# Rotary attention: a tile's three projections one behind the other, and the steps' instructions bound to the order in the source

## The chip, the cores and the metric

The kernel runs on one core of a Trainium2 chip. The metric is device time in microseconds (us), the median of several runs. The core has five engines that work side by side, each with its own queue of instructions in a fixed order: TensorE (PE in the profile, its weight loads PEld), VectorE (DVE), ScalarE (ACT), GpSimd (POOL) and SyncE (SP), which here issues transfers. A dependency between engines is a semaphore: an instruction whose input is late holds back everything behind it in its engine's queue. Results of TensorE go to PSUM, a small memory that is handed out in buffers. TensorE's clock is granted by a throttle; the profile shows it as a share of full speed (PEclk).

## What is computed

A residual stream x of 32 sequences, each 64 x 256, goes through eight blocks, alternately a form of attention or mixing and a form of feed-forward network; each adds its gated result to x. The seventh, called block 6 here since counting starts at 0, is an attention with rotary positions over 64 channels (8 heads of 8) and 256 positions, with keys and values from a second input c:

```python
def _L3_xattn_ref(x, c, Wq, bq, Wk, bk, Wv, bv, Wo, bo):
    ...
    q = split_heads(_proj(x, Wq, bq))
    k = split_heads(_proj(c, Wk, bk))
    v = split_heads(_proj(c, Wv, bv))
    q = _apply_rotary(q_emb, q)
    k = _apply_rotary(k_emb, k)
    scores = jnp.einsum('bhtc,bhsc->bhts', q, k) / math.sqrt(K_CH)
    p_attn = jax.nn.softmax(scores, axis=-1)
    out = jnp.einsum('bhts,bhsc->bhtc', p_attn, v)
    ...
    return _proj(out, Wo, bo)
...
x = x + jnp.tanh(g_xattn[3]) * _L3_xattn_ref(_layernorm(x, axis=-1), ctx_2048, ...)
x = x + jnp.tanh(g_ffn[3]) * _L3_ffn_ref(_layernorm(x, axis=-1), L3_ffn_W1, L3_ffn_W2, L3_ffn_W3)
```

The last line is block 7, a feed-forward network whose hidden values pass a Walsh-Hadamard transform; the kernel applies the transform to the weights W2 in place of the hidden values.

## The kernel before

x stays on the chip as 16 tiles of 128 rows, two sequences each. `block6` (L1102) is a generator: each `yield` ends a step, and there are 4 x 32 + 12 = 140 steps, numbered g = 0 to 139. A sequence takes four steps of scores, so a tile takes eight, and the steps are a software pipeline over several sequences:

- `start(i)` (L1150) prepares tile i: the layer norm xn (DVE), the key projection pk (8 matmuls of L1161 on ctx, into a PSUM pair), two multiplies by cosine and sine (t, L1164, DVE), their sum k and two masked copies kb (L1170, L1173, POOL); then the query projection pq from xn (also L1161) with its two multiplies and the sum q (L1177, POOL); then the value projection pv, into a small PSUM buffer of the pool `aux`, and copies into va (ACT). It yields after each of the three, and the loop at the end of `block6` takes these parts at steps with g % 8 = 1, 5 and 7, for the tile that comes next.
- `scores(w, p, g)` (L1200) does two score groups in one step. For the sequence that starts now, pp (L1219, 4 matmuls) holds scores with queries on the partitions, and DVE takes their negated maxima (mx, L1227). For the sequence six steps older, pw (L1211, 8 matmuls) holds the scores with keys on the partitions and the maximum already inside, and ACT takes the exponential e (L1223).
- `shift` (L1193) turns the four steps' maxima (pt) and adds them to the query (qs, DVE); `mix` (L1229) multiplies e with the values (po) and is called twice a sequence; `normalise` (L1239) transposes (pn), takes the reciprocal and the product o (DVE); `turn` (pot, L1251) and `finish` (py, L1258) make the output projection, and POOL adds it to x (L1263). A sequence reaches them 4, 8, 10, 11, 13 and 15 steps after its start.

PSUM limits how far steps overlap. pw, pp and the key and query projections all take a `pair` (L1127), a buffer of two banks. There are two such buffers, and a third from step 7 on; they are taken in turn, so a new pair waits until the third last one has been read.

The layer norm's mean and variance (`_stats`, L112; one `bn_stats` of L98 and one aggregate of L101 a tile, and an inverse root by 11 small operations for four tiles together) are asked for four tiles at a time: at the beginning for tiles 0 to 3, and then, in the source, one tile a step over four steps and the inverse root whole in the fifth, 14 steps ahead of each further group of four.

Steps 0 to 6 are laid between the last pieces of block 5, two steps to three pieces. The remaining ones run in the loop of `program` at L1505. That loop also takes pieces of `weights7` (L1309) at every fourth step from g = 60 on: four Hadamard products of weights (ph, PE and ACT), then butterflies of additions and subtractions on POOL between ha and hb (L1326, L1327). At g = 130 it calls `next(seventh)`, which runs `features(0)` of block 7 (L1341): statistics of tiles 0 to 3, four normalised tiles xn, eight transposes (L153) and two copies xf, with which block 7's first matmuls begin.

The order of the source is not the order of the queues. The language's scheduler takes the program's instructions and places each on its engine's queue by its own estimate of readiness; what a later block's source asks for can come to lie between the instructions of an earlier one, as long as the dependencies hold. Tiles are handed out from their pools accordingly.

Of the kernel before, what the change touches and what calls it, by code (L numbers as in the profile page):

```python
# [17 lines left out]
F32 = mybir.dt.float32  # L18
# [8 lines left out]
P = 128  # L27
B, S, D = 32, 64, 256
# [52 lines left out]
def _rsqrt(c, pool, nv, tag, bufs=1):  # L81


    nc = c.nc
    n = nv.shape[1]
    r, t = (pool.tile([P, max(n, 4)], F32, tag=f"{tag}_{m}", name=f"{tag}_{m}", bufs=bufs)[:, :n] for m in "rt")
    nc.vector.tensor_scalar(r.bitcast(I32), nv.bitcast(I32), -0.5, GUESS, ALU.mult, ALU.add)
    for _ in range(3):
        nc.vector.tensor_tensor(t, r, r, ALU.mult)
        nc.vector.tensor_tensor(t, t, nv, ALU.mult)  # L90
        nc.vector.scalar_tensor_tensor(r, t, 1.5, r, ALU.add, ALU.mult)
    return r

# [10 lines left out]
def _inverse(c, pool, mv, tag, bufs=1):  # L104

    n = mv.shape[1]
    nv = pool.tile([P, max(n, 4)], F32, tag=f"{tag}_nv", name=f"{tag}_nv", bufs=bufs)[:, :n]
    c.nc.vector.tensor_scalar(nv, mv[:, :, 1], 1e-5, -0.5, ALU.add, ALU.mult)
    return _rsqrt(c, pool, nv, tag, bufs)

# [991 lines left out]
def block6(c):  # L1102
# [7 lines left out]
    nc = c.nc  # L1110
    HN, HC = 8, 8
# [8 lines left out]
    with ExitStack() as es:  # L1120
# [29 lines left out]
        def start(i):  # L1150

            xn = _norm(c, tp, lns[i // 4], i, bufs=2)
            ctx = c.ctx.rearrange("p k t -> p (k t)")[:, i * D : (i + 1) * D]

            def project(w, src, n):

                pp = pair("pp")
                for r in range(2):
                    for m in range(2):
                        rows = slice(m * S, (m + 1) * S)  # L1160
                        nc.tensor.matmul(pp[:, m, r, :], w[rows, r, :], src[rows, :], start=True, stop=True)  # L1161
                t = [tp.tile([P, 2, D], F32, tag=f"t{r}", name=f"t{r}") for r in range(2)]
                for r, f in enumerate((cos, sin)):
                    nc.vector.scalar_tensor_tensor(t[r], pp[:, :, r, :], bias[:, n, r : r + 1], f, ALU.add, ALU.mult)  # L1164
                return t

            a = [SimpleNamespace(i=i, n=n, e={}, mx=mxs[n]) for n in range(2)]
            t = project(wk, ctx, 1)
            k = tp.tile([P, 2, D], F32, tag="k", name="k", bufs=1)
            nc.gpsimd.tensor_tensor(k, t[0], t[1], ALU.add)  # L1170
            kb = tp.tile([P, 2, 2, D], F32, tag="kb", name="kb", bufs=3)
            for h in range(2):
                nc.gpsimd.tensor_scalar(kb[:, :, h, :], k, odd[:, h : h + 1], None, ALU.mult)  # L1173
            yield a
            t = project(wq, xn, 0)
            q = tp.tile([P, 2, D], F32, tag="q", name="q", bufs=3)
            nc.gpsimd.tensor_tensor(q, t[0], t[1], ALU.add)  # L1177
            yield a
            pv = ps1.tile([P, 2, P], F32, tag="a", name="pv")
            for j in range(2):  # L1180
                nc.tensor.matmul(pv[:, j, :], ctx[:, j * P : (j + 1) * P], wv, start=True, stop=True)
            va = vas[i % 3]
            o = tp.tile([P, 2, 2, S], F32, tag="o", name="o")
            for n in range(2):
                src = pv[:, :, n * S : (n + 1) * S].rearrange("p k (h d) -> p k h d", d=HC)
                nc.scalar.copy(va[:, n, :, :, :HC], src)
                a[n].q, a[n].k, a[n].v, a[n].o = q[:, n], kb[:, n], va[:, n], o
            yield a
# [77 lines left out]


        lns = [_stats(c, sm, 0, 4, bufs=2)]
        seqs = []
        for g in range(4 * B + 12):  # L1270
            at = lambda back: seqs[(g - back) // 4] if g >= back and (g - back) // 4 < B else None
            first = lambda back: at(back) if (g - back) % 4 == 0 else None
            if g == 0:
                seqs += list(start(0))[-1]
            scores(at(6), at(0), g)
            if a := first(8):
                mix(a, 0)
# [8 lines left out]
            if (a := first(15)) and a.n:  # L1286
                finish(a)
            if g // 8 + 1 < B // 2 and g % 8 in (1, 5, 7):
                if g % 8 == 1:
                    parts = start(g // 8 + 1)  # L1290
                fresh = next(parts)
                if g % 8 == 7:
                    seqs += fresh

            ahead = g - 32 * len(lns) + 14
            if len(lns) < 4 and ahead >= 0:
                if ahead == 0:
                    mv = sm.tile([P, 4, 2], F32, tag="ln_mv", name="ln_mv", bufs=2)
                if ahead < 4:
                    _mean(c, sm, mv[:, ahead, :], 4 * len(lns) + ahead)  # L1300
                else:
                    lns.append((mv, _inverse(c, sm, mv, "ln", 2), 4 * len(lns)))
            yield
# [72 lines left out]
def program(tc, a, out):  # L1376
    nc = tc.nc
    with ExitStack() as es:
# [122 lines left out]
        with ExitStack() as es6:  # L1501
            c.third = es6.enter_context(tc.tile_pool(name="ps6b", bufs=1, space=PSUM))
            ha = es6.enter_context(tc.tile_pool(name="ha7", bufs=1)).tile([P, NH, D], F32, tag="ha", name="ha")
            w2s = weights7(c, ha, hb)
            for _ in sixth:  # L1505
                if g >= 60 and g % 4 == 0:
                    next(w2s, None)
                if g == 4 * B + 2:
                    next(seventh)
                g += 1  # L1510
        next(seventh, None)
# [119 lines left out]
```

## Time and profile before

| quantity | value |
|---|---|
| median of 3 runs | 1457.77 us (1457.44 to 1458.16) |
| profiled execution | 1453.52 us |
| its span | 1451.7 us |
| mean granted TensorE clock | 0.934 |
| block 6's exps (L1223) | 128 of 1.024 us each |
| block 6's maxima (L1227) | 128 of 1.219 us each |
| eight matmuls of one projection (L1161) | 1.06 us from the first one's start to the next group's |
| first matmul of block 7 (L1361) | at 1279.45 us |

The span goes from the first to the last instruction of the profiled execution; its own time, 1453.52 us, has 1.8 us around that. In the profile's rows the arrow `pw<-qs,kb` says that an instruction writes pw from qs and kb; x with a number is how many instructions are put together; brackets give the idle time of the engine just before, and what ended it. The timeline's columns are start, length, engine, line, operation, names and shapes. The windows give, for a stretch of time, the busy time of each engine with its number of instructions, the granted clock, the share of the transfer engines and what they moved.

### The profile page before, as it was taken

The page shows a single profiled execution, that of the slowest core. Times are in us where ns is not written, and L with a number is a line of the kernel's source. Part 1 is how long each engine was busy: PE and PEld are TensorE (multiplying, and loading weights), DVE is VectorE, ACT ScalarE, POOL GpSimd, SP SyncE. Part 2 cuts the span into 40 slices and gives each one's busy share as a digit, 9 for nine tenths or more (in the row PEclk, how much of TensorE's full clock was granted, in tenths as well). Part 3 has the DMA queues.
Part 4 walks back from the last instruction along what each step waited for, and adds up shares of the span by engine and source line. Part 5 has one row for each costly group of instructions (what it writes and reads, how often), then busy time and mean ns, then how long its engine had stood idle before and what let it go on. Part 6 is the DMA issues. An engine that isn't in the chain of part 4 may idle for free.

```text
span 1451.7 us, 21390 instructions
## 1 busy us (share of the span) xinstructions
PE 1265.6 (87%) x8342; PEld 745.8 (51%) x8342; DVE 930.1 (64%) x2189; ACT 619.1 (43%) x1044; POOL 448.9 (31%) x466
## 2 busy tenths in 40 slices
PE   1889989999879999778888874899899899999999
PEld 1666445455223677555555552455455455546665
DVE  5679685643378877686888778677776677532111
ACT  2554451312311455566777762255455354531110
POOL 3352442301131323344555455233135332100000
PEclk9999999999999999887998887699899899999999
DMA  5000000100530200000000010200000000000000
GB/s 202 15 7 9 1 1 11 48 0 8 196 116 1 95 1 1 1 1 1 2 1 1 1 60 0 87 2 1 1 2 1 1 1 2 1 0 15 15 15 14
DMA packets 10293, 34.12 MB, mean 24 GB/s; under 512 B 1360, under 2 KB 5968, under 8 KB 8528
## 3 DMA queue, kind: packets, MB, share of 16 engines
q1 hardware_dynamic: 10192, 32.76, 6.3%
q8 instruction: 65, 1.06, 0.3%
q14 instruction: 36, 0.29, 0.1%
HBM read 30.66 MB, written 2.10 MB: 23 GB/s over the span
## 4 chain that ended last, share of the span: by engine, by line
PE 55%; DVE 25%; POOL 9%; issue 4%; ACT 4%; DMA 2%; SPq 0%; POOLq 0%; DVEq 0%; ACTq 0%
PE pw L1211 5%; PE po L1371 4%; PE pg L1361 4%; PE pu L1361 4%; PE pp L1219 4%; PE pc L581 4%; PE po L1234 3%; POOL kb L1173 2%; DVE mx L1227 2%; PE pq L806 2%; PE pu L434 2%; PE pg L434 2%; PE pm L1061 2%; PE pu L437 2%; DMA w<-in_l2f 2%
## 5 line engine op out<-in xcount | busy, mean ns | idle before, releaser
L1223 ACT ACTIVATE e<-pw 128x1024 f32<-128x1024 f32 x128 | 131.0, 1024 | 175.5 <-PE pp L1219 171.5
L1227 DVE TENSOR_REDUCE mx<-pp 128x4 f32<-128x1024 f32 x128 | 156.0, 1219 | 77.4 <-PE pp L1219 77.4
L1211 PE MATMUL pw<-qs,kb 32*128 32x256 f32 x1024 | 159.0, 415 | 7.0 <-DVE mx L1227 7.0
L1219 PE MATMUL pp<-kb,q 32*128 32x512 f32 x512 | 153.7, 676 | 7.5 <-DVE mx L1227 5.0
L1211 PEld LDWEIGHTS pw<-qs,kb 32*128 32x128 f32 x1024 | 88.3, 188 | 49.5 <-issue 26.6
L581 PE MATMUL pc<-xw,wb 64*64 64x512 f32 x768 | 93.3, 619 | 0.2 <-DVE x L514 0.2
L440 ACT ACTIVATE sg<-pg 128x512 f32<-128x512 f32 (+1 forms) x75 | 37.8, 511 | 115.9 <-PE pg L434 50.5
L98 DVE BATCH_NORM_STATS2 ln_st<-x 128x6 f32<-128x256 f32 x128 | 51.0, 411 | 38.2 <-POOL x L1263 27.6
L1364 DVE TENSOR_TENSOR h<-pu,sg 128x512 f32<-128x512 f32 x32 | 22.1, 691 | 80.8 <-PE pu L1361 80.8
L441 DVE TENSOR_TENSOR h<-pu,sg 128x512 f32<-128x512 f32 (+1 forms) x75 | 42.5, 573 | 48.3 <-PE pu L434 30.0
L1234 PE MATMUL po<-e,va 128*32 128x256 f32 x1024 | 70.6, 395 | 1.2 <-ACT e L1223 1.2
L1363 ACT ACTIVATE sg<-pg 128x512 f32<-128x512 f32 x32 | 19.1, 597 | 122.8 <-PE pg L1361 122.7
L732 POOL TENSOR_TENSOR acc<-acc,sq 128x512 f32<-128x512 f32 x28 | 39.4, 1408 | 69.8 <-ACT sq L731 68.4
L581 PEld LDWEIGHTS pc<-xw,wb 64*64 64x64 f32 x768 | 29.8, 138 | 59.6 <-issue 58.8
L1361 PE MATMUL pg<-xf,wa 128*128 128x512 f32 x128 | 60.3, 592 | 0.0
L1361 PE MATMUL pu<-xf,wa 128*128 128x512 f32 x128 | 60.3, 592 | 0.0
L1170 POOL TENSOR_TENSOR k<-t,t 128x512 f32<-128x512 f32 x16 | 20.3, 1266 | 123.4 <-DVE t L1164 123.4
L1371 PE MATMUL po<-hb,h 128*128 128x256 f32 x256 | 55.9, 379 | 0.0
L1066 POOL TENSOR_TENSOR v<-v,wb 128x512 f32<-128x512 f32 x32 | 40.6, 1274 | 42.7 <-ACT v L1065 42.5
L1371 PEld LDWEIGHTS po<-hb,h 128*128 128x128 f32 x256 | 48.6, 190 | 8.3 <-issue 1.9
L139 DVE TENSOR_SCALAR xn<-x,ln_mv,ln_r 128x256 f32<-128x256 f32 x112 | 49.5, 474 | 4.9 <-PE pt L153 4.1
L1219 PEld LDWEIGHTS pp<-kb,q 32*128 32x128 f32 x512 | 41.0, 192 | 22.4 <-DVE mx L1227 16.5
(337 smaller groups left out, 3012.8 us busy)
## 6 DMA issues: line engine op xcount, KB each, us to landing
w<-in_l2f SPq DMA_DIRECT2D x12, 512.0 KB, 4.4
wa<-in_l0f SPq DMA_DIRECT2D x2, 1828.0 KB, 12.2
wa<-in_l1f SPq DMA_DIRECT2D x2, 1536.0 KB, 9.2
wa<-in_l3f SPq DMA_DIRECT2D x2, 1536.0 KB, 8.1
wb<-in_conv SPq DMA_DIRECT2D x1, 2048.0 KB, 7.6
ctx<-in_ctxT SPq DMA_DIRECT2D x2, 1024.0 KB, 6.2
ctx<-in_ctxN SPq DMA_DIRECT2D x2, 1024.0 KB, 6.0
out<-x SPq DMA_DIRECT2D x16, 128.0 KB, 1.7
```

The costliest lines, as they stand in the source:

```text
L98: ins = c.nc.vector.bn_stats(st, c.x[:, i, :])
L139: c.nc.vector.tensor_scalar(xn, c.x[:, i, :], mv[:, j, 0:1], rs[:, j : j + 1], ALU.subtract, ALU.mult)
L434: nc.tensor.matmul(p, wt[:, k, fc], xf[:, k, :N], start=k == 0, stop=False, skip_group_check=True)
L441: nc.vector.tensor_tensor(h[s][:, f, :], pu, sg, ALU.mult)
L581: nc.tensor.matmul(pcs[h][to], w[rows, k, m, h, :], xw[rows, k, h, :, Z - m : Z - m + 32], start=m == 0, stop=m == Z)
L1211: nc.tensor.matmul(pw[:, jj, k, :], w.k[rows, h, k * P : (k + 1) * P], w.qs[rows, :], start=True, stop=True)
L1219: nc.tensor.matmul(pp[:, jj], p.q[rows, t * P : (t + 1) * P], p.k[rows], start=True, stop=True)
L1223: nc.scalar.activation(e, pw, AF.Exp, scale=scale)
L1227: nc.vector.tensor_reduce(p.mx[:, t, i0 : i0 + 2, 16:18], pp, AX.X, ALU.max, negate=True)
L1234: nc.tensor.matmul(po[strip(j), :], a.v[:, k, 2 * j + h, :], a.e[h, j][:, k, :], start=k == 0, stop=k == 1)
L1361: nc.tensor.matmul(p, wt[:, k, fc], xf[:, k, :], start=k == 0, stop=k == 1)
L1371: nc.tensor.matmul(po, h[:, f, q * P : (q + 1) * P], c.w2h[:, f, :], start=f == 0, stop=f == NH - 1)
```

## The change

The projections of a tile are issued together. `start(i)` yields once after its layer norm, taken at g % 8 = 1, and then does pk, pv and pq directly one behind the other at g % 8 = 3, right after that step's scores and ahead of its `mix`, `shift`, `normalise`, `turn` and `finish`. The value projection takes a `pair` in place of the small buffer. The multiplies, sums and copies follow the three.

The statistics come in single pieces: `stats6` does one tile, or one round of the inverse root, a step; it begins 18 steps ahead of its group's first step in place of 14.

The loop over the rest of block 6, with the pieces of `weights7` and the call of `next(seventh)`, stands in `tc.manual_schedule` for PE, DVE, ACT and POOL: these engines' instructions from there keep the order of the source. SP is not in the list. No operation is added or left out.

```diff
@@ -81,15 +81,21 @@
 def _rsqrt(c, pool, nv, tag, bufs=1):
+    return [r for r in _rsqrt_slowly(c, pool, nv, tag, bufs)][-1]
+
+
+def _rsqrt_slowly(c, pool, nv, tag, bufs=1):
+
     nc = c.nc
     n = nv.shape[1]
     r, t = (pool.tile([P, max(n, 4)], F32, tag=f"{tag}_{m}", name=f"{tag}_{m}", bufs=bufs)[:, :n] for m in "rt")
     nc.vector.tensor_scalar(r.bitcast(I32), nv.bitcast(I32), -0.5, GUESS, ALU.mult, ALU.add)
     for _ in range(3):
+        yield None
         nc.vector.tensor_tensor(t, r, r, ALU.mult)
         nc.vector.tensor_tensor(t, t, nv, ALU.mult)
         nc.vector.scalar_tensor_tensor(r, t, 1.5, r, ALU.add, ALU.mult)
-    return r
+    yield r
 def _mean(c, pool, mv, i, here=False):
@@ -103,10 +109,14 @@
 def _inverse(c, pool, mv, tag, bufs=1):
+    return [r for r in _inverse_slowly(c, pool, mv, tag, bufs)][-1]
+
+
+def _inverse_slowly(c, pool, mv, tag, bufs=1):
     n = mv.shape[1]
     nv = pool.tile([P, max(n, 4)], F32, tag=f"{tag}_nv", name=f"{tag}_nv", bufs=bufs)[:, :n]
     c.nc.vector.tensor_scalar(nv, mv[:, :, 1], 1e-5, -0.5, ALU.add, ALU.mult)
-    return _rsqrt(c, pool, nv, tag, bufs)
+    yield from _rsqrt_slowly(c, pool, nv, tag, bufs)
 def _stats(c, pool, i0=0, n=NT, bufs=1, here=False):
@@ -1149,41 +1159,48 @@
         def start(i):
+
             xn = _norm(c, tp, lns[i // 4], i, bufs=2)
             ctx = c.ctx.rearrange("p k t -> p (k t)")[:, i * D : (i + 1) * D]
-
-            def project(w, src, n):
+            yield
+
+            def project(w, src):
                 pp = pair("pp")
                 for r in range(2):
                     for m in range(2):
                         rows = slice(m * S, (m + 1) * S)
                         nc.tensor.matmul(pp[:, m, r, :], w[rows, r, :], src[rows, :], start=True, stop=True)
+                return pp
+
+            def rotate(pp, n):
+
                 t = [tp.tile([P, 2, D], F32, tag=f"t{r}", name=f"t{r}") for r in range(2)]
                 for r, f in enumerate((cos, sin)):
                     nc.vector.scalar_tensor_tensor(t[r], pp[:, :, r, :], bias[:, n, r : r + 1], f, ALU.add, ALU.mult)
                 return t
             a = [SimpleNamespace(i=i, n=n, e={}, mx=mxs[n]) for n in range(2)]
-            t = project(wk, ctx, 1)
+            pk = project(wk, ctx)
+            pv = pair("pv").rearrange("p a b d -> p (a b d)")[:, : 2 * P].rearrange("p (j o) -> p j o", j=2)
+            for j in range(2):
+                nc.tensor.matmul(pv[:, j, :], ctx[:, j * P : (j + 1) * P], wv, start=True, stop=True)
+            pq = project(wq, xn)
+            va = vas[i % 3]
+            for n in range(2):
+                src = pv[:, :, n * S : (n + 1) * S].rearrange("p k (h d) -> p k h d", d=HC)
+                nc.scalar.copy(va[:, n, :, :, :HC], src)
+            t = rotate(pk, 1)
             k = tp.tile([P, 2, D], F32, tag="k", name="k", bufs=1)
             nc.gpsimd.tensor_tensor(k, t[0], t[1], ALU.add)
             kb = tp.tile([P, 2, 2, D], F32, tag="kb", name="kb", bufs=3)
             for h in range(2):
                 nc.gpsimd.tensor_scalar(kb[:, :, h, :], k, odd[:, h : h + 1], None, ALU.mult)
-            yield a
-            t = project(wq, xn, 0)
+            t = rotate(pq, 0)
             q = tp.tile([P, 2, D], F32, tag="q", name="q", bufs=3)
             nc.gpsimd.tensor_tensor(q, t[0], t[1], ALU.add)
-            yield a
-            pv = ps1.tile([P, 2, P], F32, tag="a", name="pv")
-            for j in range(2):
-                nc.tensor.matmul(pv[:, j, :], ctx[:, j * P : (j + 1) * P], wv, start=True, stop=True)
-            va = vas[i % 3]
             o = tp.tile([P, 2, 2, S], F32, tag="o", name="o")
             for n in range(2):
-                src = pv[:, :, n * S : (n + 1) * S].rearrange("p k (h d) -> p k h d", d=HC)
-                nc.scalar.copy(va[:, n, :, :, :HC], src)
                 a[n].q, a[n].k, a[n].v, a[n].o = q[:, n], kb[:, n], va[:, n], o
             yield a
@@ -1265,14 +1282,27 @@
+        def stats6(i0):
+            mv = sm.tile([P, 4, 2], F32, tag="ln_mv", name="ln_mv", bufs=2)
+            for j in range(4):
+                _mean(c, sm, mv[:, j, :], i0 + j)
+                yield
+            yield from (None if r is None else (mv, r, i0) for r in _inverse_slowly(c, sm, mv, "ln", 2))
+
         lns = [_stats(c, sm, 0, 4, bufs=2)]
-        seqs = []
+        seqs, more = [], None
         for g in range(4 * B + 12):
             at = lambda back: seqs[(g - back) // 4] if g >= back and (g - back) // 4 < B else None
             first = lambda back: at(back) if (g - back) % 4 == 0 else None
             if g == 0:
                 seqs += list(start(0))[-1]
             scores(at(6), at(0), g)
+            if g // 8 + 1 < B // 2:
+                if g % 8 == 1:
+                    parts = start(g // 8 + 1)
+                    next(parts)
+                if g % 8 == 3:
+                    seqs += next(parts)
             if a := first(8):
                 mix(a, 0)
             if a := first(10):
@@ -1285,21 +1315,14 @@
                 turn(a)
             if (a := first(15)) and a.n:
                 finish(a)
-            if g // 8 + 1 < B // 2 and g % 8 in (1, 5, 7):
-                if g % 8 == 1:
-                    parts = start(g // 8 + 1)
-                fresh = next(parts)
-                if g % 8 == 7:
-                    seqs += fresh
-
-            ahead = g - 32 * len(lns) + 14
-            if len(lns) < 4 and ahead >= 0:
-                if ahead == 0:
-                    mv = sm.tile([P, 4, 2], F32, tag="ln_mv", name="ln_mv", bufs=2)
-                if ahead < 4:
-                    _mean(c, sm, mv[:, ahead, :], 4 * len(lns) + ahead)
-                else:
-                    lns.append((mv, _inverse(c, sm, mv, "ln", 2), 4 * len(lns)))
+
+            if len(lns) + (more is not None) < 4 and g == 32 * len(lns) - 18:
+                more = stats6(4 * len(lns))
+            if more:
+                ln = next(more)
+                if ln:
+                    lns.append(ln)
+                    more = None
             yield
@@ -1502,12 +1525,14 @@
             c.third = es6.enter_context(tc.tile_pool(name="ps6b", bufs=1, space=PSUM))
             ha = es6.enter_context(tc.tile_pool(name="ha7", bufs=1)).tile([P, NH, D], F32, tag="ha", name="ha")
             w2s = weights7(c, ha, hb)
-            for _ in sixth:
-                if g >= 60 and g % 4 == 0:
-                    next(w2s, None)
-                if g == 4 * B + 2:
-                    next(seventh)
-                g += 1
+
+            with tc.manual_schedule(engines={mybir.EngineType.PE, mybir.EngineType.DVE, mybir.EngineType.Activation, mybir.EngineType.Pool}):
+                for _ in sixth:
+                    if g >= 60 and g % 4 == 0:
+                        next(w2s, None)
+                    if g == 4 * B + 2:
+                        next(seventh)
+                    g += 1
         next(seventh, None)
```

## The prediction

> **What bounds the kernel now.** I first read the shares, the clock row, the chain of waits and the costliest groups of the page.
>
> ```profile
> PE 1265.6 (87%) x8342; PEld 745.8 (51%) x8342; DVE 930.1 (64%) x2189; ACT 619.1 (43%) x1044; POOL 448.9 (31%) x466
> PEclk9999999999999999887998887699899899999999
> PE 55%; DVE 25%; POOL 9%; issue 4%; ACT 4%; DMA 2%; SPq 0%; POOLq 0%; DVEq 0%; ACTq 0%
> L1223 ACT ACTIVATE e<-pw 128x1024 f32<-128x1024 f32 x128 | 131.0, 1024 | 175.5 <-PE pp L1219 171.5
> L1227 DVE TENSOR_REDUCE mx<-pp 128x4 f32<-128x1024 f32 x128 | 156.0, 1219 | 77.4 <-PE pp L1219 77.4
> ```
>
> TensorE leads with 87%, but DVE is on the chain for a quarter of the span, and the clock is below nine tenths in six slices, 20 to 28 with gaps: the stretch of the rotary attention (about 885 to 1279 us), the only block that the change touches. There I read 20-us windows.
>
> ```profile
> core 0: us, PE busy (x) PEld busy (x) DVE busy (x) ACT busy (x) POOL busy (x), PEclk, DMA share, GB/s
> ...
> 1120.00:1140.00 20.00, 13.22 (x114) 6.74 (x112) 11.34 (x26) 6.23 (x8) 12.57 (x9) 0.76 0.00 1
> ...
> 1160.00:1180.00 20.00, 19.64 (x196) 10.55 (x192) 14.41 (x21) 10.21 (x17) 6.14 (x6) 1.00 0.01 2
> ```
>
> The block normally keeps TensorE full at full clock (second row); at single places it falls out of step and pays twice, for the idle and for the clock after it (first row). The timeline of that place:
>
> ```profile
> 1123.90 2.36 POOL L1327 TENSOR_TENSOR hb<-ha 128x1024 f32<-128x1024 f32 x1
> ...
> 1126.22 1.27 POOL L1170 TENSOR_TENSOR k<-t,t 128x512 f32<-128x512 f32 x1
> ...
> 1127.59 3.10 POOL L1173 TENSOR_SCALAR kb<-k,con 128x512 f32<-128x512 f32 x2
> 1130.66 0.72 POOL L1263 TENSOR_TENSOR x<-x,y 128x256 f32<-128x256 f32 x1
> 1131.41 0.43 DVE L98 BATCH_NORM_STATS2 ln_st<-x 128x6 f32<-128x256 f32 x1 [6.56 <-POOL x L1263]
> ...
> 1134.64 1.65 PE L1161 MATMUL pp<-xn,wb 64*128 64x256 f32 x6 [6.74 <-DVE mx L1227]
> ```
>
> Butterflies of the next block's weights bunch on POOL, so the residual x is late; the statistics queued on DVE wait for it, the maxima stand behind them, and TensorE is idle for 6.74 us.
>
> I measure the block by the start of each tile's key projection (L1161, first of eight matmuls). The undisturbed distance is 20.30 us (1050.89 to 1071.19; 1147.02 to 1167.32; 1167.32 to 1187.62). The others are longer by 2.8 (1002.26 to 1025.39), 5.2 (to 1050.89), 3.2 (1071.19 to 1094.68), 3.2 (to 1118.18), 8.5 (to 1147.02) and 1.8 (to 1230.02).
>
> **Change, part 1: what the fixed order removes.** In the changed program's instruction queues, as built, the statistics come one tile a step, the butterflies lie behind the tile's k, kb, q and x instead of bunched ahead of them, and the next block's features no longer lie between the maxima. So four excesses go: 2.8 + 5.2 + 8.5 + 1.8 = 18.3. The two of 3.2 hold two ph (Hadamard) groups each, some 1.6 a group because they split a step's scores; their matmuls remain, about 1.1 by the eight-matmul groups of this size, so 2 x (3.2 - 2.2) = 2.0 more. Sum 20.3. The work itself stays. DVE is busy 14.41 of 20 us in the window above, which covers statistics of four tiles (4 x (0.43 + 0.18) + 11 x 0.2 = 4.6) over eight steps and no more; POOL, at 6.14 of 20, covers two butterflies of up to 2.36. Without that cover each costs its own length once. I take 18.5; bounds 12 (every statistics batch delays one maximum, three of 2.8) and 20.3.
>
> **Part 2: the three projections together.** A step is two score groups (1.06 together); its exp starts 0.18 after them, lasts 1.02, and its PSUM pair is free 0.06 later, so the next step's second group starts 1.26 after the scores' end, or, where the maximum holds the pair, after 0.12 + 1.22 + 0.06 = 1.40. Pure steps thus take 1.26 + 1.06 = 2.32. Rows of the block's end, where no projection is left:
>
> ```profile
> 1252.11 1.02 ACT L1223 ACTIVATE e<-pw 128x1024 f32<-128x1024 f32 x1 [1.10 <-PE pp L1219]
> 1253.19 0.70 PE L1219 MATMUL pp<-kb,q 32*128 32x512 f32 x2
> 1254.48 1.02 ACT L1223 ACTIVATE e<-pw 128x1024 f32<-128x1024 f32 x1 [1.04 <-PE pp L1219]
> 1255.56 0.70 PE L1219 MATMUL pp<-kb,q 32*128 32x512 f32 x2
> 1256.79 1.02 ACT L1223 ACTIVATE e<-pw 128x1024 f32<-128x1024 f32 x1 [0.79 <-PE pp L1219]
> ```
>
> Each step hence has 1.26 us that TensorE must fill with something. Before, the key projection (1.06), the query projection (1.06) and the value projection (0.54) fill such holes of three different steps. Afterwards all stand behind the scores of step 3 of 8: pk 1.06 to 1.06; pv, which now takes a PSUM pair, waits for that step's exp until 1.31, and ends at 1.85; pq 1.06 to 2.91; pn and py, 0.50 + 0.52, to 3.93; next scores 1.06: 4.98. The other seven steps by the same rule: 2.43, 2.38, 2.32, 2.45, 2.32, 2.32, 2.38. Sum 21.58, and I add 0.22 for the one release in three that is the maximum's, later by 0.14, in the emptied steps. So 21.8 - 20.3 = 1.5; rounded down to 1.4, because the 20.30 has such waits already in part. Thirteen tiles (steps 19 to 115): **+18.2**. Bounds: 0.8 a tile (the seven free steps at 2.32 and nothing more: 16.2 + 4.98 = 21.2), so 10.4, and 1.9 (the four rotary multiplies, 4 x 0.70, now in a row on DVE, delay one maximum by half a microsecond), so 24.7. pv on a pair costs nothing in itself: its 0.25 wait is counted.
>
> **Part 3: the first steps,** laid between the last pieces of the block before. There the old order has a burst of statistics on DVE between two maxima (931 to 935), TensorE idle 2.35 at 930.77 and half clock behind it; steps 6 to 8 took 8.28 us (end of scores 930.25 to 938.53). At the rule's pace they take 4.6: -3.7. Steps 8 to 17 (938.53 to 961.21, 22.68) hold one lump: 23.5, +0.8. The four statistics that DVE ran ahead of step 6's end move back as well, 4 x 0.39, -1.5. Sum **-4.4**; bounds -7 (half clock gone up to step 6 too) and -2 (the idle comes back at another step).
>
> **Part 4: the last steps.** The next block's features are asked for at step 130, and now their statistics and normalisation stay there. Before, they were done early (xn at 1037 to 1039), and their transposes started at 1270.67, 6.5 after the scores of step 127 (1264.16), waiting for nothing. In the changed DVE queue 12 statistics, 8 aggregates and 17 small operations stand between the last shift add and the four normalisations. The add ends at 1267.71, 3.5 after the same point. 12 x 0.40 (successive rows at 930.75, 931.12, 931.52) = 4.8, and of the 25 small ones (0.2 apart where dependent) between 1.8, most slipping in between, and 4.2: 6.6 to 9.0. First normalised tile 10.1 to 12.6 after step 127, TensorE ready at 6.5, and its transposes stand ahead of step 131's scores: idle 4 to 6. An idle this long also costs clock. After the idle of 1.56 at 1016.24, windows show 0.50 in 1018 to 1020, 0.68 in 1020 to 1022, then 1.00: 4 us at about half, some 2 us lost. Together **+7.2**; bounds 4 (no clock lost) and 10. [...]
>
> **Part 5: waits that the trace can't show.** Queues now bound to the source may let a late producer block what a scheduler had put around it, above all x on POOL behind kb (3.10) and q. Between 0 and 5 (one idle like that of 1038); as POOL is idle two thirds of the time I take 1.
>
> Sum: -18.5 + 18.2 - 4.4 + 7.2 + 1 = +3.5 on the profiled execution's 1453.52 us, 1457.0; the median of the runs lies 4.25 above that, so **1461.3**.
>
> **Rivals.** *(A) The lump fits and the repairs win: faster.* One mechanism, at step 3 of 8: the other seven steps run at their bare 2.32, since the tail rows above do. The price is then 0.8 a tile in place of 1.4, 13 x 0.6 = 7.8 less: **1453.5**. It decides below 1.4 - 3.5/13 = 1.13 a tile. For it: pure steps at 2.31 to 2.37 in the rows. Against: the steps with pot, mix and shift stand at 2.45 there. *(B) The lump upsets DVE.* Four multiplies, a reciprocal and the o product run before the next maximum; that, and each pair held by it, makes step 4 late as well, 1.9 a tile or 6.5 more in all: **1467.8**. For it: DVE on the chain for 25%. Against: by the sum above the multiplies end at 4.43 and o at 5.0, about when that maximum's scores end. *(C) The change doesn't do what it says,* that is, the scheduler's order was this one already: 1457.8. The queues as built differ, so this has little.
>
> **How the numbers follow.** Forecast (a few microseconds slower, own range 1457 to 1466) 0.47; A 0.28; B 0.21; C 0.04. A measurement of this kernel tells about 0.2%, 2.9 us, from no change. The forecast's case puts a quarter of itself within that, A a fifth, C all: same 0.22. Faster is four fifths of A with a little of the forecast's lower edge, 0.26; slower 0.52. The range runs from A's middle less two, 1451, to B's upper half, 1469.
>
> **What would show it.** Right: the key projections 21.5 to 22 apart without 5 to 9 us exceptions; no window near 0.76 clock between 1000 and 1240; the transposes of the next block's xn preceded by a TensorE idle of 4 to 6 us, released by DVE. Wrong: distances of 21.1 or less (A), idle before pw or pp named by the maximum at step 4 or 5 (B), or transposes without a wait (part 4 falls, 7 us less).

## The result and the profile after

The changed kernel takes 1463.87 us (median of 15 runs, 1458.63 to 1465.64); the kernel before, run beside it, 1455.91 (15 runs). The ratio is 1.0057, 95% interval 1.0042 to 1.0071: slower by 0.6%, some 8 us. The forecast was +3.5 us, 1461.3, in a range of 1451 to 1469. The direction is as forecast and the time lies in the range, but the loss is 8 us where 3.5 were forecast.

The page of the changed kernel, the same three rows as shown of before and the two groups of exps and maxima:

```profile
PE 1268.5 (87%) x8342; PEld 741.6 (51%) x8342; DVE 933.8 (64%) x2189; ACT 621.2 (42%) x1044; POOL 446.3 (31%) x466
PEclk9899999999999999887988987999999999989999
PE 60%; DVE 21%; ACT 6%; POOL 5%; issue 4%; DMA 2%; SPq 0%; ACTq 0%; POOLq 0%; DVEq 0%
L1244 DVE TENSOR_REDUCE mx<-pp 128x4 f32<-128x1024 f32 x128 | 156.5, 1223 | 94.6 <-PE pp L1236 93.1
L1240 ACT ACTIVATE e<-pw 128x1024 f32<-128x1024 f32 x128 | 131.0, 1023 | 144.6 <-PE pp L1236 137.5
```

Counted from 1, slices 26, 29 and 32 stood at 6, 8 and 8 before; these dips are gone, slice 25, at the block's start, is at 7 as before, and one new dip stands at slice 36. DVE's share of the chain fell from 25% to 21% and POOL's from 9% to 5%; TensorE and ACT took it over. Windows of the two stretches that the prediction showed, or their like:

```profile
core 0: us, PE busy (x) PEld busy (x) DVE busy (x) ACT busy (x) POOL busy (x), PEclk, DMA share, GB/s
1120.00:1140.00 20.00, 18.81 (x180) 9.80 (x172) 14.94 (x24) 9.69 (x15) 9.03 (x9) 1.00 0.01 2
1180.00:1200.00 20.00, 18.68 (x188) 9.56 (x184) 13.12 (x17) 9.68 (x15) 9.30 (x8) 1.00 0.01 2
```

The first window, once 13.22 us busy at a clock of 0.76, is now as good as any other. But the usual window is worse: 18.7 of 20 us busy (second row) in place of 19.64. The change traded rare long stalls for a short one in every tile.

The distances of a tile's key projections say it in numbers. After: 22.05 us on average in ten undisturbed tiles (21.83 to 22.31), 24.54 and 24.41 where Hadamard products are in between, one of 22.67. Before: 20.30, with six distances longer than that, by up to 8.5.

The second loss is at the end, where the timeline of the changed kernel (TensorE alone) shows:

```profile
1269.27 1.07 PE L1251 MATMUL po<-e,va 128*32 128x256 f32 x16
1274.01 2.21 PE L163 MATMUL pt<-ident,xn 128*128 128x128 f32 x8 [3.67 <-DVE xn L149]
```

TensorE stands for 3.67 us before the transposes of block 7's first normalised tiles, because DVE runs 12 statistics and their small operations first. And the clock then stays down, by windows of the same run:

```profile
1273.00:1275.00 2.00, 0.99 (x4) 0.67 (x5) 2.00 (x13) 0.00 (x0) 0.00 (x0) 0.67 0.00 0
1275.00:1277.00 2.00, 2.00 (x10) 1.58 (x11) 1.45 (x11) 0.58 (x1) 0.00 (x0) 0.50 0.00 0
...
1283.00:1285.00 2.00, 2.00 (x18) 1.01 (x12) 0.09 (x1) 0.57 (x2) 0.00 (x0) 0.50 0.00 0
...
1289.00:1291.00 2.00, 2.00 (x8) 0.94 (x5) 0.00 (x0) 0.37 (x1) 0.00 (x0) 0.56 0.00 0
1291.00:1293.00 2.00, 2.00 (x10) 0.89 (x8) 0.55 (x2) 0.37 (x1) 0.00 (x0) 1.00 0.00 0
```

Half clock for some 17 us, though TensorE counts as busy in nearly all of it (all but one idle of 1.18 us). It ends only after block 7's matmuls have begun (1289.32).

Profiled executions differ by the time they reach the rotary attention: its first maximum comes anywhere between 902.4 and 910.0 us. So I compare lengths inside it: from the first maximum to the last (mx, step 0 to step 127), and from there to block 7's first matmul (pg).

| kernel | first to last maximum | last maximum to pg | sum |
|---|---|---|---|
| before | 355.75 | 15.17 | 370.92 |
| after | 353.88 | 25.45 | 379.33 |

The sum is 8.4 us longer, which is what the medians show. The steps themselves came out 1.9 us shorter, the tail 10.3 longer.

### The profile page after: what moved, and what is told of

It reads as the page before. It is cut to its first block, busy times and chain, and to the rows that moved or that the text cites. A ratio compares the mean times of both kernels' runs of the same rounds, so it can differ in the third digit from the quotient of the medians.

```text
span 1462.3 us, 21403 instructions
## 1 busy us (share of the span) xinstructions
PE 1268.5 (87%) x8342; PEld 741.6 (51%) x8342; DVE 933.8 (64%) x2189; ACT 621.2 (42%) x1044; POOL 446.3 (31%) x466
## 4 chain that ended last, share of the span: by engine, by line
PE 60%; DVE 21%; ACT 6%; POOL 5%; issue 4%; DMA 2%; SPq 0%; ACTq 0%; POOLq 0%; DVEq 0%
PE pp L1236 6%; PE pw L1228 5%; PE po L1251 4%; PE pg L1384 4%; PE po L1394 4%; PE pu L1384 4%; PE pc L591 4%; ACT e L1240 2%; PE pq L816 2%; PE pm L1071 2%; PE pu L444 2%; PE pg L444 2%; PE pu L447 2%; DVE mx L1244 2%; DMA w<-in_l2f 2%
## 5 line engine op out<-in xcount | busy, mean ns | idle before, releaser
L1236 PE MATMUL pp<-kb,q 32*128 32x512 f32 x512 | 143.8, 641 | 25.5 <-DVE mx L1244 12.6
L1228 PEld LDWEIGHTS pw<-qs,kb 32*128 32x128 f32 x1024 | 83.9, 186 | 36.4 <-issue 30.3
L1195 POOL TENSOR_TENSOR k<-t,t 128x512 f32<-128x512 f32 x16 | 20.3, 1270 | 219.5 <-DVE t L1180 219.5
L1251 PEld LDWEIGHTS po<-e,va 128*32 128x32 f32 x1024 | 27.1, 110 | 53.8 <-issue 35.4
L1076 POOL TENSOR_TENSOR v<-v,wb 128x512 f32<-128x512 f32 x32 | 40.5, 1272 | 42.6 <-ACT v L1075 42.4
```

Source lines behind the costliest of these rows:

```text
L1076: nc.gpsimd.tensor_tensor(v[:, cols], v[:, cols], vb[:, cols], ALU.add)
L1228: nc.tensor.matmul(pw[:, jj, k, :], w.k[rows, h, k * P : (k + 1) * P], w.qs[rows, :], start=True, stop=True)
L1236: nc.tensor.matmul(pp[:, jj], p.q[rows, t * P : (t + 1) * P], p.k[rows], start=True, stop=True)
L1251: nc.tensor.matmul(po[strip(j), :], a.v[:, k, 2 * j + h, :], a.e[h, j][:, k, :], start=k == 0, stop=k == 1)
```

## The experiments

The question was what the parts of the change are worth: the lump (three projections at one step), the fixed order, the statistics in pieces, the pair for pv, and the tail. All runs with their ratios to the kernel before:

| run | median us | ratio to before (95%) | first to last maximum | to pg |
|---|---|---|---|---|
| e1_stats_early | 1469.1 | 1.0108 (1.0079 to 1.0137) | 373.52 | 15.17 |
| e2_spread | 1443.1 | 0.9919 (0.9891 to 0.9947) | 334.80 | 25.20 |
| e3_spread_stats_early | 1441.41 | 0.9907 (0.9878 to 0.9936) | 344.48 | 15.18 |
| e4_lump_free_order | 1521.54 | 1.0467 (1.0443 to 1.0491) | 421.89 | 15.17 |
| e5_order_alone | 1436.18 | 0.9883 (0.9856 to 0.9909) | 331.25 | 25.46 |
| e6_early_bound | 1450.73 | 0.9989 (0.9971 to 1.0007) | 354.76 | 15.18 |
| e7_spread_early_bound | 1438.7 | 0.9901 (0.9867 to 0.9935) | 338.11 | 15.18 |
| e8_pv_small | 1458.05 | 1.0030 (1.0012 to 1.0048) | 349.52 | 25.45 |
| e9_order_late_stats | 1431.01 | 0.9840 (0.9805 to 0.9874) | 330.94 | 15.17 |
| e10_spread_pv_pair | 1433.02 | 0.9850 (0.9805 to 0.9896) | 324.73 | 25.44 |
| e11_lump_step1 | 1457.59 | 1.0020 (0.9995 to 1.0045) | 350.48 | 25.45 |
| e12_all | 1424.01 | 0.9818 (0.9799 to 0.9838) | 327.33 | 15.17 |

### The tail: e1 and e6

In `block7`, statistics of tiles 0 to 3 in pieces ahead of `features`:

```diff
+        mv = sm.tile([P, 4, 2], F32, tag="e_mv", name="e_mv")
+        for j in range(4):
+            _mean(c, sm, mv[:, j, :], j)
+            yield
+        for r in _inverse_slowly(c, sm, mv, "e"):
+            if r is not None:
+                c.early = (mv, r, 0)
+            yield
...
-            pts = _normT(c, sm, c.aux, _stats(c, sm, 4 * t, 4, bufs=2), t, "a")
+            pts = _normT(c, sm, c.aux, c.early if t == 0 else _stats(c, sm, 4 * t, 4, bufs=2), t, "a")
...
-                    if g == 4 * B + 2:
+                    if 100 <= g < 108 or g == 4 * B + 2:
```

> The changed kernel with one thing moved: the statistics of block 7's first four tiles and their inverse root are taken one piece a step in steps 100 to 107; normalisation, transposes and copies stay at step 130. Theory (the stall before those transposes is DVE's statistics): the TensorE idle of 3.67 us before the transposes shrinks below 0.8, the clock stays at 1.00 from 1260 to 1290, and the first matmul of block 7 starts 15.5 us after the last maximum as in the kernel before, not 25.4; time about 10 us below the changed kernel, so 2 us below the kernel before. Rival (the tail is slow for other reasons of the fixed order, such as the output projection ahead of the scores): at most 5 us of the 10 return. Steps 100 to 107 may lose up to 0.5 us each if DVE has no room; I expect none.

The tail did what the theory said: 15.17 us, the old value to the hundredth. But the run is slower than the changed kernel, by 5 us in the medians and by 9.4 in the two stretches, and no theory had that: the steps take 19.6 us more, 18.0 of them from step 100 on. The timeline at step 104, DVE and TensorE:

```profile
1200.14 0.40 DVE L104 BATCH_NORM_STATS2 ln_st<-x 128x6 f32<-128x256 f32 x1
1200.45 0.17 DVE L107 BATCH_NORM_AGGREGATE ln_mv<-ln_st 128x2 f32<-128x6 f32 x1
1200.54 0.40 DVE L104 BATCH_NORM_STATS2 ln_st<-x 128x6 f32<-128x256 f32 x1
...
1203.69 0.70 PE L1228 MATMUL pw<-qs,kb 32*128 32x256 f32 x4 [1.09 <-DVE qs L1215]
...
1205.47 1.22 DVE L1244 TENSOR_REDUCE mx<-pp 128x4 f32<-128x1024 f32 x1
...
1206.74 0.70 PE L1236 MATMUL pp<-kb,q 32*128 32x512 f32 x2 [2.35 <-DVE mx L1244]
```

The statistics there write ln_mv, not e_mv: they belong to block 7's later groups of tiles. That code stands behind the ordered part, the scheduler is free with it, and it had followed the first group up into the attention. So e6 binds those as well; `here=True` makes each of these statistics keep its place in the program (the lines are against e1):

```diff
-            pts = _normT(c, sm, c.aux, c.early if t == 0 else _stats(c, sm, 4 * t, 4, bufs=2), t, "a")
+            pts = _normT(c, sm, c.aux, c.early if t == 0 else _stats(c, sm, 4 * t, 4, bufs=2, here=True), t, "a")
```

> The changed kernel with block 7's first statistics in steps 100 to 107, as in the run before, and now the statistics of block 7's later groups of tiles bound to their place in the source as well. In the run before, eight and more of those later ones had slipped in between the maxima of steps 100 to 112. Theory (the stall before block 7's transposes costs 10 us, and only the later groups' statistics made the move cost 14): nothing lost at steps 100 to 112 (last maximum within 1 us of the changed kernel's distance), the tail 10 us shorter, about 10 us below the changed kernel, so within 3 us of the kernel before. Rival (DVE has no room in those steps for any statistics): 5 us or more lost there again.

The theory's case: the sum of both stretches is 369.94, 9.4 below the changed kernel, and the ratio to before covers 1. The steps lost 0.9 us by the early statistics, the tail gained 10.3. The windows from 1255 to 1261 us have a clock of 1.00, and behind them the groups keep the lengths that they have there: eight pw 1.13 and sixteen po 1.07 up to 1272 us, where the changed kernel has 2.08 and 1.94 after its idle. The transposes wait for nothing now:

```profile
1263.53 1.22 PE L163 MATMUL pt<-ident,xn 128*128 128x128 f32 x8
1264.22 0.59 ACT L1375 COPY xf<-pt 128x512 f32<-128x512 f32 x1 [0.18 <-PE pt L163]
```

So the stall in the tail, with the half clock that follows, is shown to cost 10.3 us. Without it the change is a draw.

### The lump and the order: e2, e4 and e5

e2 puts the projections back to their old steps under the new order (pv in the small buffer):

```diff
-            if g // 8 + 1 < B // 2:
-                if g % 8 == 1:
-                    parts = start(g // 8 + 1)
-                    next(parts)
-                if g % 8 == 3:
-                    seqs += next(parts)
...
+            if g // 8 + 1 < B // 2 and g % 8 in (1, 5, 7):
+                if g % 8 == 1:
+                    parts = start(g // 8 + 1)
+                    next(parts)
+                fresh = next(parts)
+                if g % 8 == 7:
+                    seqs += fresh
```

with a `yield a` ahead of pq and another ahead of pv in `start`.

> The changed kernel with the three projections back at steps 1, 5 and 7 of eight, the value projection in the small PSUM buffer again, everything else (fixed order, statistics in pieces) as changed. Theory (the lump costs what the cycle got longer): the distance of key projections falls from 22.1 to 20.3 us, without the long ones of the kernel before; thirteen of them make 23 us less than the changed kernel, the tail stall stays; about 1441, 15 us below the kernel before. Rival (the fixed order itself makes the cycle longer, whatever the placement): distances of 21.5 or more, and at most 8 us less than the changed kernel.

Undisturbed distances are 19.9 to 20.1, and the run is about 11 us below the kernel before: the theory's direction, some 4 us short of its size. Of what is missing, 2.5 us lie ahead of step 16 (47.16 for 44.65); the rest lies at three tiles with 21.99 or 22.66, those with the statistics in pieces beside the spread multiplies.

e4 keeps the lump and gives the order back to the scheduler (no `manual_schedule`, old statistics):

```diff
-            with tc.manual_schedule(engines={mybir.EngineType.PE, mybir.EngineType.DVE, mybir.EngineType.Activation, mybir.EngineType.Pool}):
-                for _ in sixth:
+            for _ in sixth:
...
```

> The other way round: the projections one behind the other as in the changed kernel, but the scheduler orders freely as before, and the statistics stand in the source as before. Theory (the lump costs 1.8 us a tile whoever orders, and the fixed order is what removes the long distances): undisturbed distances near 22, long ones of 5 us and more still there, no stall before block 7's transposes; about 15 to 23 us above the kernel before. Rival (a free order repairs the lump by putting steps' work between the projections): distances of 20.5 to 21, within 5 us of the kernel before.

The tail has no stall, as expected (15.17), but both sizes were far off: 68 us above the kernel before, with one distance of 21.93 and all later ones between 24.6 and 30.5. Its timeline shows the old kind of stall, now in nearly every tile:

```profile
1165.49 0.43 DVE L104 BATCH_NORM_STATS2 ln_st<-x 128x6 f32<-128x256 f32 x1 [3.58 <-POOL x L1280]
...
1170.07 0.80 PE L1228 MATMUL pw<-qs,kb 32*128 32x256 f32 x2 [5.82 <-DVE qs L1215]
```

DVE waits 3.58 us for an x that POOL adds behind kb, the maxima stand behind that, and TensorE is idle for 5.82. Between 970 and 1305 us DVE waits for x like this 13 times, about once a tile, for 2.5 to 3.6 us. That it is the lump's k and kb, one behind the other on POOL, that make x late in every tile is read from these rows; no run tried it apart.

e5 is the kernel before with the fixed order as its only edit.

```diff
-            for _ in sixth:
+            with tc.manual_schedule(engines={mybir.EngineType.PE, mybir.EngineType.DVE, mybir.EngineType.Activation, mybir.EngineType.Pool}):
+                for _ in sixth:
...
```

> The kernel before with the fixed order as its only edit: projections at steps 1, 5 and 7, statistics in the source as before (one tile a step, but the inverse root whole in one step). It differs from the run with spread projections only in the statistics in pieces. Theory (the fixed order itself removes the long distances; the pieces add little): distances near 20.1, at most three places with 1 to 3 us more where the inverse root of 11 small operations stands before a maximum, the tail stall of 10 us as in the changed kernel; 1443 to 1450. Rival (the pieces are what matters): long distances of 5 us or more remain, and it is no faster than the kernel before.

The theory held and asked too little: 0.9883, some 17 us faster, tail stall included. Distances are 19.90 to 20.10, and with statistics 20.67 twice and 21.47 once, less than with the pieces (21.99 and 22.66); the two with Hadamard products are 22.43 and 22.41. The pieces are thus a loss where the multiplies are spread: e2's steps take 3.55 us more than e5's. So the two halves of the change pull against each other. Fixing the order is worth -14.2 us by the two stretches: -24.5 in the steps and +10.3 in the tail. Everything else in the change gives 22.6 of the steps' gain back.

### What the lump costs: e8, e10 and e11

e8 is the changed kernel with pv in the small buffer again:

```diff
-            pv = pair("pv").rearrange("p a b d -> p (a b d)")[:, : 2 * P].rearrange("p (j o) -> p j o", j=2)
+            pv = ps1.tile([P, 2, P], F32, tag="a", name="pv")
```

> The changed kernel with one thing undone: the value projection takes the small PSUM buffer again, so a tile takes 18 pairs in place of 19; the place of the three projections stays. Theory (the cycle is longer because three holes stay empty and one step is overfull): the distance of key projections stays at 22 within 0.3, since the wait of 0.26 before pv goes but the pairs' turn stays as tight. Rival (the nineteenth pair shifts every later pair's release): distances of 21 or less, 13 us or more below the changed kernel.

The distance is 21.80, 0.25 shorter than in the changed kernel: the theory's case, though not the nothing that it took the pair to cost, and the steps together are 4.4 us shorter.

e8 against e2 shows where the lump's cost arises, since the two differ only in the place of the projections. A step leaves TensorE a hole of some 1.26 us in which it waits for the step's buffer unless it has other work. From one maximum to the next, the eight steps of an undisturbed tile take, in us:

| run | 0 | 1 | 2 | 3 | 4 | 5 | 6 | 7 | sum |
|---|---|---|---|---|---|---|---|---|---|
| e2, projections at 1, 5 and 7 | 2.45 | 2.83 | 2.44 | 2.37 | 2.44 | 2.47 | 2.45 | 2.45 | 19.90 |
| e8, all three at 3 | 2.45 | 2.46 | 2.31 | 4.86 | 2.44 | 2.37 | 2.46 | 2.45 | 21.80 |

Step 3 pays 2.49 for the lump, and the emptied steps give back only some 0.6 (0.37 at step 1, 0.13 at step 2, 0.10 at step 5, nothing at step 7): most of the work had been free where it stood.

e10 makes the opposite edit to e2, pv on a pair where the projections are spread (the two diff lines above, reversed).

> The earlier run with spread projections, and only the value projection on a pair there too (19 pairs a tile in place of 18). Theory (the nineteenth pair costs about 0.3 us a tile by itself, as between the changed kernel and the one with the small buffer): distances longer by 0.2 to 0.4, 3 to 5 us more than that run. Rival (it cost only because of the wait for the exp inside the lump, which is absent here): within 1.5 us of that run.

Both expectations failed. The run is 10 us faster than e2 by the steps (324.73 against 334.80), with undisturbed distances of 19.38 to 20.00, and 19.78, 22.07 and 20.58 at the three tiles with statistics (e2: 21.99, 21.99 and 22.66). The nineteenth pair is no cost in itself; it costs in the lump, where pv stands between pk and pq and waits, and helps in the spread order. With 18 pairs a tile and three buffers, each step meets the same buffer in every tile; with 19 the turn shifts by one, and in e10 the distances recur every three tiles (19.99, 19.48, 19.38). In the undisturbed tiles the gain lies at two steps in two tiles of three: 1.98 for 2.44 after the key projection (step 2), and 2.31 for 2.45 after the query projection (step 6). Another 2.5 us of the 10 lie ahead of step 16. Why the turn of the buffers does this was not tried further. It also means that the lump has no single price: it costs 14.7 us of the steps with pv in the small buffer (e8 less e2) and 29.2 with pv on a pair (changed kernel less e10).

e11 moves the lump from step 3 to step 1:

```diff
-            if g // 8 + 1 < B // 2:
-                if g % 8 == 1:
-                    parts = start(g // 8 + 1)
-                    next(parts)
-                if g % 8 == 3:
-                    seqs += next(parts)
+            if (g + 1) // 8 + 1 < B // 2:
+                if g == 0 or g % 8 == 7:
+                    parts = start((g + 1) // 8 + 1)
+                    next(parts)
+                if g % 8 == 1:
+                    seqs += next(parts)
```

> The changed kernel with the lump of three projections at step 1 of eight in place of step 3, the layer norm at step 7 before. Step 1 also holds only the turn of the output (0.44 us), where step 3 holds two groups (1.02). Theory (the lump costs what overflows its own step's hole of 1.26 us while other holes stay empty): the distance falls from 22.1 to 21.4 or 21.6, about 8 us below the changed kernel, tail stall unchanged. Rival (the lump's cost is the four multiplies in a row on DVE, or pairs, whichever step holds it): distances of 22 or more.

The theory's lower figure for the distance: 21.34 to 21.41. The number of multiplies and pairs is the same as at step 3, so the 0.65 that went are not theirs: step 1 holds one group of 0.44 beside the lump, step 3 two of together 1.02. What overflows the hole of its own step is paid, and nothing else fills the other holes. The time fell less than the 8 expected, 3.4 us by the two stretches: from step 16 on it is the 8.3 (300.91 for 309.23), but the steps ahead of it took 49.57 us for 44.65, which the theory did not have. The steps of the changed kernel at the lump, TensorE and what pv waits for:

```profile
1187.96 1.13 PE L1173 MATMUL pp<-ctx,wb 64*128 64x256 f32 x8
...
1189.35 0.71 PE L1187 MATMUL pv<-wb,ctx 128*128 128x128 f32 x4 [0.26 <-DVE mx L1244]
1189.99 1.14 PE L1173 MATMUL pp<-xn,wb 64*128 64x256 f32 x8
...
1191.06 0.66 PE L1262 MATMUL pn<-ident,po_sb 128*128 128x128 f32 x4
1191.55 0.60 PE L1277 MATMUL py<-oT,wb 128*128 128x256 f32 x2
1192.08 0.48 PE L1228 MATMUL pw<-qs,kb 32*128 32x256 f32 x2
...
1193.15 1.07 PE L1251 MATMUL po<-e,va 128*32 128x256 f32 x16
```

From the lump's start to the end of the next scores it is 5.19 us. In two tiles of three pv waits 0.18 for the exp (e) in place of 0.26 for the maximum, and it is 5.11. Meanwhile a step with a hole left unfilled waits like this:

```profile
1196.90 0.70 PE L1236 MATMUL pp<-kb,q 32*128 32x512 f32 x2 [0.81 <-ACT e L1240]
```

0.81 us idle, for the exp, in the step where the query projection stood before.

### Putting the parts together: e3, e7, e9 and e12

e3 joins e1's and e2's edits, e7 those of e6 and e2.

> Both edits of the two other runs together. Theory (two separate costs in different places): the gains add up, 33 us below the changed kernel, about 1430 us and 1.7% below the kernel before. Rival (they share a cause): less than 25 us below the changed kernel.

> The same two edits with the projections spread over steps 1, 5 and 7. Theory: the gains of both add up now, 20 + 10 us below the changed kernel: 1430 to 1434 us, about 1.5% below the kernel before. Rival: the early statistics collide with the multiplies, which here lie in three steps: 1438 or more.

Both theories missed, and both times the rival's figure came out: e3 is 22 us below the changed kernel, e7 at 1438.7. In e3 the cause is e1's fault, later groups among the maxima, and no shared one. In e7 those are bound, and still 3.3 us of the tail's 10 are lost again (338.11 against e2's 334.80), by the rival's mechanism: the distance is 22.71 where the early statistics stand beside spread multiplies. So e9 takes them in steps 120 to 127, where no multiply is left, and block 6's own statistics as before the change:

```diff
-                    if 100 <= g < 108 or g == 4 * B + 2:
+                    if 120 <= g < 128 or g == 4 * B + 2:
```

> Fixed order, projections spread over steps 1, 5 and 7, block 6's own statistics as in the kernel before (one tile a step, inverse root whole), block 7's first statistics in steps 120 to 127, where no rotary multiplies are left on DVE, and the later groups' bound. Theory (tail stall, statistics in pieces beside three spread multiplies, and early statistics in crowded steps were each a cost of its own): distances as in the run with the order alone, no loss in steps 116 to 127, first matmul of block 7 about 15.5 us after the last maximum: 10 us below the run with the order alone, about 1427, 1.9% below the kernel before. Rival (the statistics delay the last maxima wherever they stand): 4 us or less below that run.

Steps 330.94, tail 15.17: 10.6 us below e5 by the profiles. By ratio it is 0.9840 (0.9805 to 0.9874), where 1.9% less was expected; that interval still overlaps e5's. e12 adds pv on a pair:

> The best run so far (fixed order, projections at steps 1, 5 and 7, block 7's first statistics in steps 120 to 127, later groups bound) with the value projection on a pair. Theory (on a pair the value projection makes the spread cycle shorter by 0.3 us, as between the two runs with and without it, and that is independent of the tail): about 4 us below the best run, 1427, 1.8 to 1.9% below the kernel before. Rival (that difference was chance of the single profile or of the statistics' places): within 1.5 us of the best run.

1424.01 us, ratio 0.9818 (0.9799 to 0.9838): the fastest, 27 us below the kernel before in the same session and 40 below the changed kernel across sessions. By its profile it is 3.6 us below e9 (342.50 against 346.11), the size that the theory said, but not by its account of 0.3 a tile: 2.7 of it lie ahead of step 16. Their ratio intervals overlap, so that last step alone isn't certain.

## Why the prediction was right, and where not

**The direction, the two losses and the repairs were right.** Each place that the prediction named shows in the profile: distances near 22 without exceptions of 5 to 9 us, a clock of 1.00 in each 20-us window from 1000 to 1240, the transposes behind an idle released by DVE. The sizes were not: +8.4 in the two stretches for +3.5. The lump came out 4.6 us dearer and the tail 3.1, while the other three terms together came out 2.8 lower, so part of the error cancelled; and a range of 1451 to 1469 also held the times of A (1453.5) and B (1467.8), so that the time alone tells little between them.

**What the order removes.** Forecast -18.5. The excess over the undisturbed distance from the key projection at 941.35 to the one at 1230.02 was 288.67 - 13 x 20.30 = 24.8. In the changed kernel it is 292.16 (939.97 to 1232.13) - 13 x 22.05 = 5.5, nearly all of it the Hadamard products. So -19.3. One gain the prediction did not have: by e5 the fixed order shortens the undisturbed tile too, from 20.30 to 19.91; against that figure the lump costs more than the term below says.

**The lump, the step that was mis-sized.** Forecast 1.4 a tile, measured 22.05 - 20.30 = 1.75, in all 13 x 1.75 = 22.8 for 18.2. Of the missing 0.35, 0.10 is the rounding of 1.5 down "because the 20.30 has such waits already in part", which had no row behind it and went the wrong way. Some 0.16 lies in the lump's step, 5.11 to 5.19 for 4.98 reckoned: between pk and pq the value projection took 0.64 (1189.35 to 1189.99), not the 0.54 that it took ahead of scores. The rest is in the other seven steps, 2.31 to 2.54 each and 16.9 together for 16.82 with the 0.22 added. The pair is no part of it: "its 0.25 wait is counted" holds, since without the pair (e8) the distance is 0.25 shorter. The step table and e11 confirm the reckoning by holes.

**The first steps.** Forecast -4.4. From the maximum of step 0 to that of step 16 it is 954.64 - 909.99 = 44.65 us, before 958.88 - 908.53 = 50.35: -5.7.

**The tail.** Forecast +7.2, measured 10.3 (e6). The idle was 3.67, below the 4 to 6 reckoned, because small operations ran between the statistics almost for free: statistics and small operations took 6.23 us (1267.22 to 1273.45), 0.4 under the lower of the two sums. The clock term was the wrong one: "4 us at about half, some 2 us lost" was read from one event at 1016 to 1022, and the half clock lasted 17 us here. Taking the idle from the 10.3 leaves, as an estimate, 6.6 for it.

**Waits that the trace couldn't show.** Forecast +1. From the maximum of step 16 to that of step 127 it is 309.23 us, before 305.39: +3.8, where the order and the lump give -19.3 + 22.8 = 3.5. So 0.3 is left over, and -5.7 + 3.8 + 10.3 is the 8.4 of the two stretches.

**Rivals.** A needed 1.13 or less a tile and is out at 1.75. (Its price was also mis-added: 21.2 - 20.3 is 0.9 a tile, not 0.8.) B's price, 1.9 a tile, is near the measured one, but not by its mechanism: the maximum after the lump starts at 1193.27, 0.12 after its scores end (1193.15), as the 0.12 of the reckoning. C is out, since the long distances went. What none of them considered is that the two halves can be had apart: the fixed order by itself gains, and the lump loses under either order.

**A misreading.** The clock row has ten slices below nine tenths and not six; of the twelve slices of the rotary attention, 25 to 36, they are 25, 26, 29 and 32. No term was worked out from it.

## What to carry to other kernels

When a pipeline's step has a hole that the slowest release sets (1.26 us here), small independent pieces of work belong one to a hole; gathered at one step they overflow it, and the other holes stay empty (in e8 the step with the lump paid 2.49 us, and the emptied ones gave back 0.6). The order bound by hand removed the stalls of a scheduler's bad guesses (24.5 us of the steps in e5), but it also nailed down what the scheduler had rightly pulled forward (10.3 us of the tail): look for every call inside the bound region that used to run early, and for free work behind it that can slip in. And measure the parts of a change apart: here the order was worth 14 us with its tail stall in it, and the lump cost 15 to 29, depending on where the value projection was put.

## What had not been expected of the hardware

After an idle of 3.67 us TensorE's clock stayed at 0.50 for some 17 us, with TensorE counted busy in all but 1.2 of the 16 us from 1275 to 1291, whereas after an idle of 2.35 us in e1 (before 1206.74) it was back at 1.00 in the window from 1211, some 4 us later. The granted clock in e1:

```profile
1206.00:1207.00 1.00, 0.26 (x4) 0.26 (x8) 1.00 (x3) 0.00 (x0) 0.00 (x0) 1.00 0.00 0
1207.00:1208.00 1.00, 1.00 (x8) 0.06 (x4) 0.41 (x4) 0.00 (x0) 0.00 (x0) 0.72 0.00 0
...
1210.00:1211.00 1.00, 1.00 (x14) 0.89 (x12) 0.00 (x0) 0.37 (x1) 0.00 (x0) 0.57 0.00 0
1211.00:1212.00 1.00, 1.00 (x16) 0.62 (x10) 0.42 (x1) 0.31 (x1) 0.00 (x0) 1.00 0.00 0
```

By such windows, with both ends worked out from the shares, the half clock lasted 3.4 us there (1207.44 to 1210.86), 3.4 in the kernel before after its idle of 1.56 (1017.88 to 1021.28, from 0.97 in 1016 to 1018 and 0.68 in 1020 to 1022), and 17.1 here (1273.68 to 1290.76), five times that. The length of the idle alone doesn't give the length of the half clock in these runs. At the kernel before's idle of 6.74 us, up to 1134.64, it lasted 10.2 (0.76 in 1130 to 1131, 0.50 up to 1140, 0.62 in 1140 to 1141), and at the changed kernel's idle of 1.66, up to 971.52, every window of 1 us from 968 to 978 has 1.00. What kept the clock down for 17.1 us here was not tried.
